# Norms of queries and keys: a maximum on VectorE and a power on GpSimd in place of Relu, Ln and Exp on ScalarE

## The chip, the core and the metric

The kernel runs on one NeuronCore of a Trainium2 chip. The metric is the device time of one launch in microseconds (us). The core has five engines with an instruction queue each, worked off in order: TensorE (PE, matmuls and transposes; PEld is its loading of weights), VectorE (DVE), ScalarE (ACT), GpSimd (POOL) and SyncE (SP, which here issues nearly all DMAs). All data are fp32.

## The reference

The input x is 4 sequences of 512 tokens with 128 channels. Six blocks follow each other, each with a layer norm ahead of it and a residual around it: a token-shift feed-forward block, global attention with 16 heads of 64 and a position bias, the feed-forward block again, then a two-layer local transformer, a gated linear recurrence, and the local transformer again with the same weights. What matters here is in the local transformer, in each of its two layers:

```python
def l2norm(t):
    return t / jnp.clip(jnp.linalg.norm(t, axis=-1, keepdims=True), 1e-12)

def _layer(x, wqkv, qs, ksc, wo, lg, lb, w1, b1, w2, b2):
    ...
    q, k, v = (to_heads(q), to_heads(k), to_heads(v))
    q = l2norm(q) * qs
    k = l2norm(k) * ksc
    q, k = rotary_xpos(q, k)
    o = local_attention(q, k, v)
    ...
...
x = x + 0.5 * _L1_ffn_ref(_layernorm(x, axis=-1), ...)
x = x + _L1_attn_ref(_layernorm(x, axis=-1), ...)
x = x + 0.5 * _L1_ffn_ref(_layernorm(x, axis=-1), ...)
```

A query or key of one head (64 numbers) is divided by its length. With 8 heads that makes 16 lengths per token. Local attention looks at windows of 64 tokens and the window before.

## The kernel before

The kernel does not write its instructions in the order in which they run. Every call on an engine is recorded first (`Recorder`, and `Plan.record`), with the tiles it reads and writes, a cost in us for the planner (`cost=` where the line gives one, else a formula in `Recorder.cost`), and a due time `plan.vt` that the program sets by hand. `Plan.plan` then walks through a model of the five queues: it takes, of the operations whose inputs are there, the one that can start first, and among those of nearly equal start the one with the earliest due time. It also hands out buffers: 33 pairs of 128x1040 floats in SBUF (each can be used as two halves), 24 small tiles of 128x16, 8 tiles for values, and 8 PSUM banks ("S"). It prices a change of the TensorE array shape and of ScalarE's function table: Exp and Ln are in one table, Gelu and Sigmoid in two others, and every change is an ACT_TABLE_LOAD (L288). `emit` writes the instructions in the planned order and pins that order on each queue. So all recorded instructions have line 318 in the profile, and groups are told apart by tile names: `pair` (halves and pairs), `small`, `psS` (PSUM), `xT` (a sequence, channels on partitions), `va` (values), `via` (a DRAM bounce buffer), and constants by their names, such as `tiny`.

A change of one cost therefore changes the order of much else: what follows in the plan, and which buffer each tile gets.

The work has three stages. The first feed-forward block runs over the 4 sequences. Global attention runs over 8 pairs of heads times 4 sequences, up to about 430 us. From there on, per sequence and overlapping each other in a staggered way: the second feed-forward block, `local_stage` (two layers), `recurrence`, `local_stage` again, `leave`.

`local_attention` works on 4 tiles of 128 tokens, pipelined by hand: in step k, `rotate(k)`, `values(k)`, `turn(k-2)`, `soften(k-3)`, `turn_back(k-5)`, `weigh(k-6)`, `turn_outputs(k-7)`, `project(k-8)`. There are 4 sequences x 2 stages x 2 layers x 4 tiles = 64 calls of `rotate`.

In `rotate` TensorE projects queries and keys (two matmuls of 512 columns), ScalarE squares them out of PSUM, and VectorE multiplies them out of PSUM by the cosine and the sine table into `u` and `w`. POOL adds the halves of the squares (L712), VectorE sums over each head into `rn`, a small tile of 128x16 (L713). Then comes the inverse length: L715 to L717, three ScalarE instructions on `rn`. POOL meanwhile adds the rotated halves of `w` to `u` (L718, L719, two instructions of 512 elements), and multiplies `u` by `rn`, spread over the 64 channels of a head (L721, 1024 elements). `turn` transposes that product for the attention matmuls: queries on TensorE, keys by 32x32 blocks on VectorE and through DRAM.

The three instructions compute exp(-0.5 ln(relu(s - 1e-24) + 1e-24)) for the sum of squares s, that is max(s, 1e-24) to the power of -1/2. The biases come from a constant tile `tiny` of two columns, set by two POOL memsets (L471 to L473).

Of the kernel before, what the change touches and what calls it, by code (L numbers as in the profile page):

```python
# [8 lines left out]
AF = mybir.ActivationFunctionType  # L9
ALU = mybir.AluOpType  # L10
# [4 lines left out]
P = 128  # L15
# [16 lines left out]
DEPTH, H1, DH, WIN = 2, 8, 64, 64  # L32
# [396 lines left out]
def tile_macaron(ctx: ExitStack, tc: tile.TileContext, i: dict, out: bass.AP):  # L429
# [6 lines left out]
    def real(name, shape, pool=pool):  # L436
        return pool.tile(shape, FP, tag=name, name=name)
# [11 lines left out]
    pe, dve, act, pool_, dma = plan.tensor, plan.vector, plan.scalar, plan.gpsimd, plan.sync  # L449

    def const(name, shape, space=pool):
        return plan.fixed(real(name, shape, space), shape)
# [15 lines left out]
    w_v = cload("w_v", [D, D], i["L0_ffn_W_v"])  # L468
    eps = const("eps", [P, 1])
    pool_.memset(eps, EPS)  # L470
    tiny = const("tiny", [P, 2])  # L471
    pool_.memset(tiny[:, 0:1], -1e-24)
    pool_.memset(tiny[:, 1:2], 1e-24)  # L473
    ones_sb = const("ones", [P, P])
    pool_.memset(ones_sb, 1.0 / D)

# [207 lines left out]
    def local_attention(l, h):  # L684
# [5 lines left out]
        def rotate(t):  # L690

            sq = plan.tile("pair", [P, 2 * INNER])
            u = plan.tile("pair", [P, 2 * INNER])
            w = plan.tile("pair", [P, 2 * INNER])
            u4 = u.rearrange("p (g h d) -> p g h d", g=2, d=DH)
            w4 = w.rearrange("p (g h d) -> p g h d", g=2, d=DH)
            for g in range(2):
                c = slice(g * INNER, (g + 1) * INNER)
                pq = plan.tile("S", [P, INNER])
                pe.matmul(pq, lhsT=h[:, t * P : (t + 1) * P], rhs=wqkv[:, c], start=True, stop=True)  # L700
                act.activation(sq[:, c], pq, AF.Square)
                p3 = pq.rearrange("p (h d) -> p h d", d=DH)
                for dst, tab in ((u, cs), (w, sn)):
                    dve.tensor_tensor(
                        dst[:, c].rearrange("p (h d) -> p h d", d=DH), p3,
                        tab[:, t, g].unsqueeze(1).to_broadcast([P, H1, DH]), ALU.mult,
                    )
            rn = plan.tile("small", [P, 2 * H1])

            s3 = sq.rearrange("p (h d) -> p h d", d=DH)  # L710
            sh = plan.tile("half", [P, 2 * H1, half])
            pool_.tensor_tensor(sh, s3[:, :, :half], s3[:, :, half:], ALU.add, cost=1.25)  # L712
            dve.tensor_reduce(rn, sh, AX.X, ALU.add)  # L713

            act.activation(rn, rn, AF.Relu, bias=tiny[:, 0:1])  # L715
            act.activation(rn, rn, AF.Ln, bias=tiny[:, 1:2])
            act.activation(rn, rn, AF.Exp, scale=-0.5)  # L717
            for lo, hi in ((slice(0, half), slice(half, DH)), (slice(half, DH), slice(0, half))):  # L718
                pool_.tensor_tensor(u4[..., lo], u4[..., lo], w4[..., hi], ALU.add, n=INNER)  # L719
            u3 = u.rearrange("p (h d) -> p h d", d=DH)  # L720
            pool_.tensor_tensor(  # L721
                u3, u3, rn.unsqueeze(2).to_broadcast([P, 2 * H1, DH]), ALU.mult, cost=1.87
            )
            us[t] = u
# [128 lines left out]
        def project(t):  # L853
# [9 lines left out]
            for rows_, cols in parts:  # L863
                c = slice(cols.start + t * P, cols.start + (t + 1) * P)
                dve.tensor_tensor(h[rows_, c], pj[rows_, :], h[rows_, c], ALU.add)


        order = (project, turn_outputs, turn_back, turn, values, rotate, soften, weigh)
        behind = {values: 0, rotate: 0, turn: 2, soften: 3, turn_back: 5, weigh: 6,
                  turn_outputs: 7, project: 8}  # L870
# [301 lines left out]
```

## Time and profile before

| | us |
|---|---|
| median of two runs (1146.81 and 1147.20) | 1147.01 |
| span of the profiled execution, first to last instruction | 1146.1 |
| busy: TensorE matmul | 1117.0 |
| busy: VectorE | 911.9 |
| busy: ScalarE | 877.0 |
| busy: GpSimd | 762.7 |
| Relu and Ln on the norms, 128 instructions, mean 309 ns | 39.6 |
| Exp on the norms, 64 instructions, mean 216 ns | 13.8 |
| function table loads, 54 instructions, mean 1283 ns | 69.3 |

The profiled execution has no time of its own beside its span; the two runs lie 0.7 and 1.1 us above that span. Busy time is the union of an engine's instructions; instructions of one engine can overlap a little, so the busy time of a group is less than its count times its mean. The idle time of a group is that of the engine just before its instructions, with the engine and the tile that ended it behind the arrow.

### The profile page before, as it was taken

How to read it: one execution, taken by the hardware profiler on the slowest of the kernel's cores; microseconds unless marked ns; L12 is line 12 of the kernel's file. 1: busy time of each engine (PE TensorE's matmuls, PEld its weight loads, DVE VectorE, ACT ScalarE, POOL GpSimd, SP SyncE). 2: the span in 40 equal slices, each digit the busy share in tenths (PEclk: the TensorE clock that was granted, in tenths of full speed). 3: DMA queues.
4: the chain of work that ended last, by engine and by line, in shares of the span. 5: the costliest groups of instructions: out<-in, count | busy, mean ns of one | idle time of the engine just before them, and what ended most of it. 6: DMA issues, size and time to landing. Idle time of an engine off the chain costs nothing.

```text
span 1146.1 us, 26884 instructions
## 1 busy us (share of the span) xinstructions
PE 1117.0 (97%) x9036; PEld 688.4 (60%) x9036; DVE 911.9 (80%) x2891; ACT 877.0 (77%) x1948; POOL 762.7 (67%) x575
## 2 busy tenths in 40 slices
PE   7999999999999999999999999999999999999997
PEld 3455656566655545557667666764457766666673
DVE  4787787868778779989788788867999978878863
ACT  5987777867787667878786788788887777777764
POOL 3675655656569459979776677523999867777610
PEclk9999999999999999999999999999999999999999
DMA  4379799797979744523432332300333423322310
GB/s 126 125 232 306 211 261 264 207 274 206 299 211 309 199 115 127 161 84 106 120 96 68 93 102 76 85 1 1 98 114 102 115 77 101 98 84 67 98 38 19
DMA packets 131613, 157.01 MB, mean 137 GB/s; under 512 B 15034, under 2 KB 101732, under 8 KB 131476
## 3 DMA queue, kind: packets, MB, share of 16 engines
q1 hardware_dynamic: 131188, 155.21, 46.4%
q8 instruction: 73, 1.20, 0.5%
q14 instruction: 64, 0.52, 0.2%
q10 hardware_dynamic: 288, 0.08, 0.0%
HBM read 78.39 MB, written 64.02 MB: 124 GB/s over the span
## 4 chain that ended last, share of the span: by engine, by line
PE 70%; DVE 13%; ACT 9%; issue 3%; POOL 2%; DMA 1%; SPq 0%; DVEq 0%; ACTq 0%; POOLq 0%
PE psS L318 70%; DVE pair L318 12%; ACT pair L318 7%; POOL pair L318 2%; DVE small L318 1%; ACT small L318 1%; DMA pair<-via 1%; ACT L288 1%; ACT va L318 1%; SPq L318 0%; DMA via<-pair 0%; DMA pair<-in_x_dram 0%; DVE xT L318 0%; DVEq L318 0%; ACTq L318 0%
## 5 line engine op out<-in xcount | busy, mean ns | idle before, releaser
L318 POOL TENSOR_TENSOR pair<-pair,small 128x1024 f32<-128x1024 f32 (+1 forms) x256 | 430.9, 1704 | 203.6 <-DVE small L318 127.7
L318 PE MATMUL psS<-pair,pair 64*64 64x128 f32 (+4 forms) x4544 | 372.5, 300 | 3.2 <-DVE small L318 1.3
L318 ACT ACTIVATE pair<-pair,small 128x128 f32<-128x128 f32 (+1 forms) x512 | 266.5, 553 | 91.7 <-DVE small L318 77.1
L318 PEld LDWEIGHTS psS<-pair,pair 128*64 128x64 f32 (+2 forms) x4544 | 252.6, 140 | 101.5 <-issue 31.3
L318 ACT COPY pair<-psS 128x512 f32<-128x512 f32 (+1 forms) x470 | 254.6, 593 | 63.5 <-PE psS L318 59.0
L318 POOL TENSOR_TENSOR pair<-pair,pair 128x512 f32<-128x512 f32 x166 | 215.2, 1309 | 109.1 <-ACT pair L318 66.8
L318 PEld LDWEIGHTS psS<-ident,pair 128*128 128x128 f32 x1488 | 171.2, 141 | 92.5 <-issue 69.9
L318 PE MATMUL psS<-ident,pair 128*128 128x128 f32 x1488 | 200.0, 275 | 9.2 <-DMA pair<-in_x_dram 5.5
L318 DVE CUSTOM_DVE_ANT_0 pair<-psS,pair 128x512 f32<-128x512 f32 x256 | 164.8, 679 | 37.1 <-PE psS L318 36.3
L318 PE MATMUL psS<-wqkv,pair 128*128 128x512 f32 x384 | 182.2, 598 | 3.4 <-DVE pair L318 3.0
L318 DVE STREAM_TRANSPOSE pair<-pair 128x512 f32<-128x512 f32 x208 | 142.8, 697 | 18.9 <-POOL pair L318 18.0
L318 POOL TENSOR_TENSOR pair<-pair 128x512 f32<-128x512 f32 x82 | 102.9, 1256 | 55.8 <-ACT pair L318 54.7
L318 PE MATMUL psS<-pair,w 128*128 128x512 f32 (+2 forms) x288 | 130.2, 595 | 0.4 <-POOL pair L318 0.2
L318 ACT ACTIVATE pair<-pair 128x512 f32<-128x512 f32 x152 | 94.5, 629 | 35.6 <-DVE pair L318 26.4
L318 DVE CUSTOM_DVE_ANT_0 pair<-psS,mask 128x128 f32<-128x128 f32 x512 | 113.9, 284 | 6.2 <-PE psS L318 4.8
L318 PE MATMUL psS<-pair 64*128 64x512 f32 x512 | 117.7, 601 | 0.0
L318 PEld LDWEIGHTS psS<-wqkv,pair 128*128 128x128 f32 x384 | 68.6, 190 | 74.6 <-issue 50.1
L318 DVE TENSOR_TENSOR pair<-psS,cos 128x512 f32<-128x512 f32 x128 | 87.2, 681 | 18.5 <-ACT pair L318 15.1
L318 DVE TENSOR_TENSOR pair<-psS,sin 128x512 f32<-128x512 f32 x128 | 87.2, 681 | 15.2 <-ACT pair L318 14.6
L318 ACT ACTIVATE pair<-psS 128x512 f32<-128x512 f32 x144 | 82.0, 596 | 18.6 <-PE psS L318 10.3
L318 PEld LDWEIGHTS psS<-pair,w 128*128 128x128 f32 (+2 forms) x288 | 50.7, 182 | 62.8 <-issue 49.5
L318 PEld LDWEIGHTS psS<-pair 64*128 64x128 f32 x512 | 48.5, 186 | 58.5 <-issue 42.0
(73 smaller groups left out, 1191.3 us busy)
## 6 DMA issues: line engine op xcount, KB each, us to landing
via<-pair SPq DMA_DIRECT2D x72, 512.0 KB, 3.8
pair<-via SPq DMA_DIRECT2D x288, 128.0 KB, 3.8
via<-pair SPq DMA_DIRECT2D x64, 256.0 KB, 2.1
pair<-via SPq DMA_DIRECT2D x256, 64.0 KB, 2.1
pair<-va SPq DMA_DIRECT2D x112, 130.0 KB, 2.3
table<-tdram SPq DMA_DIRECT2D x16, 511.5 KB, 7.2
pair<-table SPq DMA_DIRECT2D x16, 448.0 KB, 4.6
pair<-pair SPq DMA_DIRECT2D x48, 128.0 KB, 2.0
```

What stands on the lines that cost most here:

```text
L288: self.nc.scalar.add_instruction(mybir.InstLoadActFuncSet(name=self.nc.get_next_instruction_name(), engine=mybir.EngineType.Activation, ac ...
L318: real(*[a.resolve() if isinstance(a, View) else a for a in args], **{k: a.resolve() if isinstance(a, View) else a for k, a in kw.items()},)
```

## The change

The constant `tiny` gives way to a constant `power` of 128x16, filled with -0.5 by one POOL memset. In `rotate` the three ScalarE instructions give way to two: VectorE takes the maximum of `rn` and 1e-24, and GpSimd raises it, element by element, to the power in `power`. The planner is told 0.6 us for the power and its formula's value for the maximum.

```diff
@@ tile_macaron @@
-    tiny = const("tiny", [P, 2])
-    pool_.memset(tiny[:, 0:1], -1e-24)
-    pool_.memset(tiny[:, 1:2], 1e-24)
+    power = const("power", [P, 2 * H1])
+    pool_.memset(power, -0.5)
@@ rotate @@
             pool_.tensor_tensor(sh, s3[:, :, :half], s3[:, :, half:], ALU.add, cost=1.25)
             dve.tensor_reduce(rn, sh, AX.X, ALU.add)
 
-            act.activation(rn, rn, AF.Relu, bias=tiny[:, 0:1])
-            act.activation(rn, rn, AF.Ln, bias=tiny[:, 1:2])
-            act.activation(rn, rn, AF.Exp, scale=-0.5)
+            dve.tensor_scalar(rn, rn, 1e-24, None, ALU.max)
+            pool_.tensor_tensor(rn, rn, power, ALU.pow, cost=0.6)
             for lo, hi in ((slice(0, half), slice(half, DH)), (slice(half, DH), slice(0, half))):
                 pool_.tensor_tensor(u4[..., lo], u4[..., lo], w4[..., hi], ALU.add, n=INNER)
```

## The prediction

> **What bounds the kernel now.** I read the page first, then busy time by stretches, then the waits of single engines in those stretches, and last the instruction order of both kernels.
>
> ```profile
> span 1146.1 us, 26884 instructions
> PE 1117.0 (97%) x9036; PEld 688.4 (60%) x9036; DVE 911.9 (80%) x2891; ACT 877.0 (77%) x1948; POOL 762.7 (67%) x575
> ...
> POOL 3675655656569459979776677523999867777610
> ```
>
> TensorE (PE) is busy 97% of the span: only 29 us are left in which it stands still. That caps any gain from work on other engines. The POOL row says where another engine could take over: its digits are low in the first stage (the global attention) and 9 in the slices from about 430 to 545 us and from about 805 to 920 us. So I cut the local stage, which begins near 430 us, in four.
>
> ```profile
> core 0: us, PE busy (x) PEld busy (x) DVE busy (x) ACT busy (x) POOL busy (x), PEclk, DMA share, GB/s
> 430.00:545.00 115.00, 111.34 (x941) 68.05 (x940) 104.90 (x313) 92.14 (x211) 104.69 (x82) 1.00 0.40 120
> 545.00:805.00 260.00, 256.95 (x2479) 168.42 (x2478) 206.73 (x718) 206.49 (x425) 160.30 (x132) 1.00 0.24 71
> 805.00:920.00 115.00, 109.64 (x1087) 71.46 (x1087) 107.12 (x359) 93.72 (x223) 107.25 (x84) 1.00 0.38 109
> 920.00:1146.00 226.00, 217.65 (x2134) 143.78 (x2133) 165.87 (x605) 159.47 (x343) 126.33 (x102) 1.00 0.25 72
> ```
>
> The first and third rows are the dense stretches. In their 230 us PE has 9.0 us idle, POOL 18.1, DVE 18.0 and ACT 44.1. PE, POOL and DVE are all nearly full, ACT is the one with room. In the second and fourth rows PE is at 99 and 96%, and POOL has 199 us idle of 486. The granted clock is 1.00 in every row.
>
> The instructions that go, and the one that waits for them (groups of one shape):
>
> ```profile
> L318 ACT ACTIVATE small<-small,tiny 128x16 f32<-128x16 f32 x128 | 39.6, 309 | 37.2 <-DVE small L318 35.8
> ...
> L318 ACT ACTIVATE small<-small 128x16 f32<-128x16 f32 x64 | 13.8, 216 | 1.0
> ```
>
> The first group is the Relu and the Ln (two for each of 64 token tiles), the second the Exp. Between 430 and 1146 us, POOL and PE wait for them as follows (two lines from the waits of POOL, two from those of PE; columns: total us, times, longest):
>
> ```profile
> POOL pair L318 <- ACT pair L318: 90.5, 31, 17.6
> POOL pair L318 <- ACT small L318: 34.5, 23, 4.4
> ...
> PE psS L318 <- ACT pair L318: 3.4, 7, 0.7
> ...
> PE psS L318 <- ACT small L318: 0.8, 1, 0.8
> ```
>
> **What stays.** The order of both kernels is the same on PE up to the local stage; before it only two POOL memsets become one (a row of 0.10 us, within POOL idle at the start). So the first 430 us stay. From there the planner, given other costs, lays all queues out anew. The number of PE instructions is unchanged; 54 table loads stand on ACT before and after, so no table work is saved. No DMA is added, moved to another queue or dropped.
>
> **The change part by part, against the span of 1146.1 us** (0.9 under the median of 1147.0; I add 0.9 at the end).
>
> *ACT, three instructions less per tile.* 39.6 + 13.8 = 53.4 us of busy time go, and the 35.8 us for which ACT stood at the head of its queue waiting for the sum of squares. ACT has 164 us idle in these 716 us and is not the bound. What reaches the end is PE's own waiting for ACT: 3.4 + 0.8, and 0.4 for the copy of the values, 4.6 us. I take half: -2.3 us. Bounds: nothing, and -9.0, if all PE idle of the dense stretches were owed to a late ACT.
>
> *DVE, one maximum of 128x16 per tile.* No such row. The nearest are the reciprocals, 128x2 in 160 ns and 128x4 in 166 ns, and the accumulator read of 83 ns. I take 0.16 us: 64 x 0.16 = 10.2 us in all. Of 64 tiles, 27.5 have their norms in the dense stretches (26 and 29 Relu and Ln there, halved), so 27.5 x 0.16 = 4.4 us fall where DVE has 18.0 us free. Elsewhere DVE's idle of 113 us hides it. The maximum waits for the reduction on its own engine; in 15 tiles it follows it at once, and what queues behind it (PSUM evictions that PE waits for) stands for that wait; in the others one or more DVE instructions lie between, cover it, and make POOL wait longer. I take +0.7 us; bounds 0 and +4.4, with the cover gone.
>
> *POOL, one power of 128x16 per tile.* No row has this operation. From below: POOL's 128x1 multiply took 229 ns, and 15 more elements at the slope between its 128x512 and 128x1024 products by the norms, (1922 - 1048) / 512 = 1.7 ns, make 0.25 us. From above: a whole 128x1024 product, 1.92 us, that is 120 ns for each of 16 elements. The line carries the planner's figure 0.6; the same kind of figure for two other POOL lines, 1.87 and 1.25, stands beside rows of 1.92 and 1.31, within 5%. I take 0.6 us: 64 x 0.6 = 38.4 us. In the sparse stretches, 36.5 x 0.6 = 21.9 us lie in 199 us of idle and cost nothing. In the dense ones, 27.5 x 0.6 = 16.5 us meet 18.1 us of idle. Of these, 1.4 + 4.7 = 6.1 us were the wait for ACT's norm, which goes; the other 12.0 are waits for ACT's squares, DVE and PE, which stay. So 6.1 of the 16.5 are free and 10.4 press on a queue that would be 99% full (211.9 + 16.5 of 230). PE still draws on other batches there; I take half: +5.2 us. Bounds: 27.5 x 0.25 = 6.9 less 6.1, about +0.8; and 27.5 x 1.92 = 52.8 less 18.1, +34.7.
>
> What queues behind the power: in 48 of 64 tiles both additions of the rotated halves (1.31 us each) stand ahead of it and cover the reduction and the maximum, and the product by the norm comes next, which needs it anyway. The product now waits for POOL's own result; in the old trace a product starts as the additions end, without a visible gap, so I add nothing.
>
> On the choice of engine: the additions of 128x512 took 1.31 us on POOL, and two-input DVE products with both inputs in SBUF took 1.13 us for 64x512, a ratio of 1.16. [...]
>
> *PE's tile shapes change more often.* Counting runs of one array shape in the two orders, 195 become 208: 8 more of full shape, 5 of half or quarter. From the starts in the trace, 32 matmuls of 64x128 take 1.034 us and 64 take 1.907, so a run costs 2 x 1.034 - 1.907 = 0.161 us beyond its matmuls; a full-shape matmul before such a run holds the queue 0.094 us longer than its usual 0.110. So 5 x 0.161 + 8 x 0.094 = +1.6 us, on PE, hidden by nothing. Bounds 0 and +3.3 (13 x 0.25).
>
> Sum: -2.3 + 0.7 + 5.2 + 1.6 = +5.2; 1146.1 + 5.2 + 0.9 = 1152.2, rounded to **1152**. Beyond these terms the rearranged queues shift PE's idle time of 20.4 us in the local stage either way; I allow 9 us, its half in round figures.
>
> **Rivals.**
>
> *A cheaper norm path (faster, mostly within 2%).* ACT is freed on the path POOL and DVE wait on (DVE waits 45.9 us for ACT after 430 us), the planner uses it, and the dense stretches lose their PE idle: 1147.0 - 9.0 + 1.6 = 1139.6. For it: ACT's blocked 35.8 us. Against: PE waited for ACT only 4.6 us there, and the load goes to the two engines that are fuller. Over 2% faster means 23 us out of 20.4 of PE idle in the local stage, of which 8.4 lie after 920 us, mostly in the final drain: all but excluded unless matmuls that stand waiting behind each other's records are regained too.
>
> *The power is dear (slower).* In place of the Exp of L717, GpSimd needs t us for 16 powers. Once 27.5 t exceeds the 18.1 us idle, POOL sets the pace of the dense stretches, and PE, whose own work is unchanged, waits: the time is 1147.0 + 27.5 t - 18.1, plus 1.6. Slower than 2% (1170) from t = 1.5; at 1.92 it is 1183. For it: no row prices a power; POOL is at 91 and 93% there. Against: the line's 0.6.
>
> *The power blocks POOL's queue.* It waits for DVE's maximum, and if that comes late in the dense stretches by one DVE instruction of 0.68 us in each of 27.5 tiles, 18.7 us of POOL time are lost beside 16.5 of work: 35.2 - 18.1 + 1.6 = +18.7, 1165.7. Against: the covering additions in 48 tiles.
>
> **How the numbers follow.** Forecast (about 1142 to 1161): 0.57. Cheaper path (below 1142): 0.21, of which 0.04 beyond 2%. Blocked queue (about 1161 to 1170): 0.08. Dear power (above 1170): 0.14. Low end: 1132, where a tenth is left out, the forecast of the first rival less most of the 9 us; high end: 1174, t near 1.6. The bound of 2%, 1124 to 1170, is about what a measurement of this kernel can tell from no change. Faster 0.04, same 0.82, slower 0.14.
>
> **What would show it right or wrong.** A row of POOL powers x64 near 600 ns and DVE maxima x64 near 160; ACT busy near 824 us and POOL near 801; POOL above 97% busy in its two dense stretches, and PE idle there some 5 us longer; no POOL wait for ACT small in the local stage. PE idle smaller than before would refute the POOL term; powers over 1.5 us, or long waits of POOL for DVE small ahead of them, speak for the slower rivals.

## The result, and the profile after

The changed kernel takes 1267.16 us (two runs, 1264.96 and 1269.37) where the kernel before takes 1147.01: 1.104 times as long, 95% interval 1.1023 to 1.1058. The profiled execution spans 1263.2 us, 117.1 more than before. The prediction said 1152, with 1132 to 1174 as its range.

From the page of the changed kernel:

```profile
span 1263.2 us, 26806 instructions
PE 1158.3 (92%) x9036; PEld 704.5 (56%) x9036; DVE 951.3 (75%) x2955; ACT 842.8 (67%) x1756; POOL 944.6 (75%) x638
...
POOL 4667655655785699999889988229999989897920
...
L318 POOL TENSOR_TENSOR small<-small,power 128x16 f32<-128x16 f32 x64 | 187.8, 2934 | 7.6 <-DVE small L318 4.1
```

The last line is the power: 64 of them, 2934 ns each, 187.8 us in all. The busy rows say where it shows: POOL's busy time grew by 181.9 us, ScalarE's fell by 34, and TensorE, with the same 9036 instructions, has 104.9 us idle instead of 29.1. So 75.8 of the 117.1 us are TensorE standing still longer; for the other 41.3 it is busy longer with the same work, at a lower granted clock (the last section has the figures). The POOL row has turned to 8 and 9 over nearly the whole local stage, but for the slices around 820 us and the end.

On the chain of work that ended last, POOL's share went from 2% to 24% (the page before, then the page after):

```profile
PE 70%; DVE 13%; ACT 9%; issue 3%; POOL 2%; DMA 1%; SPq 0%; DVEq 0%; ACTq 0%; POOLq 0%
...
PE 47%; POOL 24%; DVE 14%; issue 6%; ACT 5%; DMA 3%; SPq 1%; POOLq 0%; DVEq 0%; ACTq 0%
```

The maximum, among the groups of VectorE:

```profile
L318 DVE TENSOR_REDUCE small<-pair 128x16 f32<-128x512 f32 x64 | 43.3, 677 | 22.6 <-POOL pair L318 22.6
L318 DVE TENSOR_SCALAR small<-small 128x16 f32<-128x16 f32 x64 | 41.9, 655 | 0.5
```

It takes as long as the reduction ahead of it, which reads 32 times as much. What PE waits for (us, times, longest; the first line is the local stage before, the others are the longest of the changed kernel):

```profile
PE psS L318 <- POOL pair L318: 0.2, 1, 0.2
...
PE psS L318 <- DVE pair L318: 33.8, 32, 3.6
PE psS L318 <- POOL pair L318: 30.1, 20, 6.0
PE psS L318 <- ACT pair L318: 15.4, 17, 2.3
```

Before, PE waited 0.2 us for POOL in the local stage; now 30.1 us, of which 23.7 us are transposes that wait for products by the norms. POOL's lateness also reaches PE through other engines: before its block transposes VectorE sat idle for POOL for 62.9 us, and for 18.0 us before the change.

### The profile page after: what moved, and what is told of

Read it like the earlier page. It is cut to its first block, busy times and chain, and to the rows that moved or that the text cites. A ratio compares the mean times of both kernels' runs of the same rounds, so it can differ in the third digit from the quotient of the medians.

```text
span 1263.2 us, 26806 instructions
## 1 busy us (share of the span) xinstructions
PE 1158.3 (92%) x9036; PEld 704.5 (56%) x9036; DVE 951.3 (75%) x2955; ACT 842.8 (67%) x1756; POOL 944.6 (75%) x638
## 4 chain that ended last, share of the span: by engine, by line
PE 47%; POOL 24%; DVE 14%; issue 6%; ACT 5%; DMA 3%; SPq 1%; POOLq 0%; DVEq 0%; ACTq 0%
PE psS L318 47%; POOL pair L318 16%; DVE pair L318 10%; POOL small L318 8%; ACT pair L318 4%; DVE small L318 3%; DMA pair<-via 1%; DMA via<-pair 1%; SPq L318 1%; DMA pair<-va 1%; DVE xT L318 1%; DMA pair<-in_x_dram 0%; DMA pair<-in_L_attn_wv_dram 0%; ACT L288 0%; POOLq L318 0%
## 5 line engine op out<-in xcount | busy, mean ns | idle before, releaser
L318 PE MATMUL psS<-pair,pair 64*64 64x128 f32 (+4 forms) x4544 | 382.1, 304 | 10.6 <-DVE pair L318 7.3
L318 PEld LDWEIGHTS psS<-pair,pair 128*64 128x64 f32 (+2 forms) x4544 | 257.1, 142 | 111.6 <-issue 28.1
L318 POOL TENSOR_TENSOR pair<-pair,pair 128x512 f32<-128x512 f32 x163 | 210.6, 1311 | 99.8 <-ACT pair L318 86.5
L318 PE MATMUL psS<-ident,pair 128*128 128x128 f32 x1488 | 215.3, 284 | 51.9 <-POOL pair L318 23.7
L318 PEld LDWEIGHTS psS<-ident,pair 128*128 128x128 f32 x1488 | 175.9, 145 | 151.6 <-issue 68.7
L318 PE MATMUL psS<-wqkv,pair 128*128 128x512 f32 x384 | 189.5, 617 | 13.5 <-DVE pair L318 7.6
L318 POOL TENSOR_TENSOR small<-small,power 128x16 f32<-128x16 f32 x64 | 187.8, 2934 | 7.6 <-DVE small L318 4.1
L318 DVE STREAM_TRANSPOSE pair<-pair 128x512 f32<-128x512 f32 x208 | 143.6, 700 | 64.0 <-POOL pair L318 62.9
L318 PE MATMUL psS<-pair,w 128*128 128x512 f32 (+2 forms) x288 | 132.9, 605 | 6.1 <-POOL pair L318 3.7
L318 POOL TENSOR_TENSOR pair<-pair 128x512 f32<-128x512 f32 x85 | 106.0, 1249 | 34.3 <-ACT pair L318 33.0
```

The lines of the kernel that those rows point to most:

```text
L318: real(*[a.resolve() if isinstance(a, View) else a for a in args], **{k: a.resolve() if isinstance(a, View) else a for k, a in kw.items()},)
```

## The experiments

Theory A: the power's time on GpSimd is the loss. The rivals: the maximum, which waits for GpSimd (B, later E); the new order of all queues (C); a plan made with a wrong cost (D).

**Four runs on the parts.**

```diff
# e1_cheap, from the changed kernel
-            pool_.tensor_tensor(rn, rn, power, ALU.pow, cost=0.6)
+            pool_.tensor_tensor(rn, rn, power, ALU.mult, cost=0.6)
# e2_honest, from the changed kernel
-            pool_.tensor_tensor(rn, rn, power, ALU.pow, cost=0.6)
+            pool_.tensor_tensor(rn, rn, power, ALU.pow, cost=2.93)
# e3_max, from the kernel before
-            act.activation(rn, rn, AF.Relu, bias=tiny[:, 0:1])
-            act.activation(rn, rn, AF.Ln, bias=tiny[:, 1:2])
+            dve.tensor_scalar(rn, rn, 1e-24, None, ALU.max)
+            act.activation(rn, rn, AF.Ln)
# e4_prices, from the kernel before, at its start (pbase filled with 0.37, pexp with -0.5)
+    for n, w in enumerate((1, 4, 16, 64)):
+        pool_.tensor_tensor(const(f"pw{n}", [P, P])[:, :w], pbase[:, :w], pexp[:, :w], ALU.pow, cost=3.0)
+    pool_.tensor_tensor(const("pwp", [P, 16])[:32, :], pbase[:32, :16], pexp[:32, :16], ALU.pow, cost=3.0)
+    pool_.tensor_tensor(const("pwone", [P, 16]), ones_sb[:, :16], pexp[:, :16], ALU.pow, cost=3.0)
+    pool_.tensor_tensor(const("pml", [P, 16]), pbase[:, :16], pexp[:, :16], ALU.mult, cost=0.3)
...
+    dve.tensor_scalar(const("vmx", [P, 16]), pbase[:, :16], 1e-24, None, ALU.max)
```

Expected of e1_cheap:

> The changed kernel with the power replaced by a product of the same two tiles, in the same order on every queue (the planner is told 0.6 us as before); the norms are then wrong in value, which no instruction's time depends on. Theory A (the power's 2.93 us on GpSimd is what costs): the product takes about 0.25 us, GpSimd's busy time falls by 64 x 2.7 = 172 us to some 772, and the time falls to 1145 to 1160. Rival B (the maximum on VectorE, which took 0.66 us on average and waits for GpSimd, is a large part): 64 x 0.5 us late, half of it felt, the time stays at 1165 to 1180. Rival C (the new order of the queues is bad by itself): the time stays above 1180.

Expected of e2_honest:

> The changed kernel with 2.93 us in place of 0.6 us as the planner's cost of the power, so that the queues are laid out for what it takes. Theory A (GpSimd has to carry 188 us more, and they stand in the chain from norm to product): GpSimd's busy time stays near 945 us, and the time stays above 1215. Rival D (most of the loss comes from a plan made for a power five times cheaper than it is): the sparse stretches, in which GpSimd had 199 us idle, take up the work and the time falls to 1165 to 1200.

Expected of e3_max:

> The kernel before with one part of the change alone: the maximum on VectorE in place of the Relu, then Ln and Exp on ScalarE as they were; no power. The maximum should again take 0.16 us where GpSimd runs nothing and up to 1.3 us where a GpSimd instruction with two inputs is running, 0.5 to 0.7 us on average. Theory A: this is a side cost, the time stays within 1140 to 1158. Rival B: 1160 to 1180.

Expected of e4_prices:

> The kernel before with powers of 1, 4, 16 and 64 elements on 128 partitions, 16 on 32 partitions, 16 of a base of 1/128, a product and a maximum of 16 elements, all on GpSimd in the first 30 us, and one maximum of 16 elements on VectorE; their results are not used. If the power is paid by the element: 0.4, 0.9, 2.9 and 11.5 us, that is (2.93 - 0.2) / 16 = 0.17 us an element, and 2.9 on 32 partitions. If it is a fixed cost of the call: all about 2.9. The product and GpSimd's maximum 0.2 to 0.3. The whole 1165 to 1175, since some 20 us come on GpSimd at the start.

Measured, with 1147.5 us for the kernel before on the same chip: e1_cheap 1172.0 us (1.0215, interval 1.02 to 1.023); e2_honest 1268.9 (1.1059, 1.1043 to 1.1076); e3_max 1174.1 (1.0228, 1.0211 to 1.0245); e4_prices 1156.6 in its one run.

The power takes 95 of the 120 us (1267.2 - 1172.0). A right cost for the planner recovers nothing, so rival D falls: POOL is busy for 946.1 us there, and the time is the same. But theory A is not all: 24.5 us stay in e1_cheap, and the maximum alone, in another order, gives 26.6. So rival B, the maximum, may be a part of the loss. The wrong values of the norms in e1_cheap do not show in the times of what is worked out from them: VectorE's block transposes take 698 ns there, 697 before the change and 700 in the changed kernel, its masked scores of 128x128 283, 284 and 283.

The price list (e4_prices, groups of POOL in the first 40 us; each ran once):

```profile
L318 POOL TENSOR_TENSOR pw<-pbase,pexp 128x64 f32<-128x64 f32 x1 | 10.5, 10543 | 0.0
...
L318 POOL TENSOR_TENSOR pwone<-ones,pexp 128x16 f32<-128x16 f32 x1 | 2.9, 2899 | 0.0
L318 POOL TENSOR_TENSOR pw<-pbase,pexp 128x16 f32<-128x16 f32 x1 | 2.9, 2897 | 0.0
L318 POOL TENSOR_TENSOR pwp<-pbase,pexp 32x16 f32<-32x16 f32 x1 | 2.9, 2891 | 0.0
L318 POOL TENSOR_TENSOR pw<-pbase,pexp 128x4 f32<-128x4 f32 x1 | 1.0, 1019 | 0.0
L318 POOL TENSOR_TENSOR pw<-pbase,pexp 128x1 f32<-128x1 f32 x1 | 0.6, 572 | 0.0
...
L318 POOL TENSOR_TENSOR pml<-pbase,pexp 128x16 f32<-128x16 f32 x1 | 0.2, 221 | 0.0
```

The power is paid by the element of a partition: from 1 to 64 elements (10543 - 572) / 63 = 158 ns each, on top of 0.41 us. The number of partitions (2891 ns on 32, 2897 on 128) and the base (2897 ns for 0.37, 2899 for 1/128) make no difference. A product of the same tiles takes 221 ns. The whole came out at 1156.6 where 1165 or more was expected, so only some 9 of POOL's 20 us at the start reached the end; why, the run does not show.

**Does the maximum wait for GpSimd?** VectorE and POOL of the changed kernel in the order of time (start, duration, in us):

```profile
576.46 0.69 DVE L318 TENSOR_REDUCE small<-pair 128x16 f32<-128x512 f32 x1 [0.54 <-POOL pair L318]
577.09 0.69 DVE L318 TENSOR_TENSOR pair<-psS,sin 128x512 f32<-128x512 f32 x1
577.70 1.22 DVE L318 TENSOR_SCALAR small<-small 128x16 f32<-128x16 f32 x1
578.84 0.68 DVE L318 TENSOR_TENSOR pair<-psS,cos 128x512 f32<-128x512 f32 x1
```

```profile
575.16 1.27 POOL L318 TENSOR_TENSOR pair<-pair 128x512 f32<-128x512 f32 x1
576.39 2.51 POOL L318 TENSOR_TENSOR pair<-pair,pair 128x512 f32<-128x512 f32 x2
579.00 2.91 POOL L318 TENSOR_TENSOR small<-small,power 128x16 f32<-128x16 f32 x1
```

The maximum starts at 577.70, just after POOL's second addition has begun, and ends at 578.92; the addition ends at 578.90. So it is in the whole trace: 11 of the 64 maxima took 158 to 196 ns, and of the 53 longer ones 52 end within 0.08 us of the end of a POOL instruction with two inputs, and the last one with a POOL memset. The additions that were to cover the chain are what holds it up: they stand ahead of the power in POOL's queue, and are running when the maximum comes.

The next four runs take this wait away without touching the order, and test order, chain and queue.

```diff
# e5_norelu, from the kernel before
-            act.activation(rn, rn, AF.Relu, bias=tiny[:, 0:1])
# e6_recip, from e3_max
-            dve.tensor_scalar(rn, rn, 1e-24, None, ALU.max)
+            dve.reciprocal(rn, rn)
...
-            act.activation(rn, rn, AF.Exp, scale=-0.5)
+            act.activation(rn, rn, AF.Exp, scale=0.5)
# e7_recip_pow, from the changed kernel
-    pool_.memset(power, -0.5)
+    pool_.memset(power, 0.5)
...
-            dve.tensor_scalar(rn, rn, 1e-24, None, ALU.max)
+            dve.reciprocal(rn, rn)
# e8_dead, from e1_cheap: a tile, and a power into it behind the product by the norms (L721)
+    dead = const("dead", [P, 2 * H1])
...
+            plan.ops[-1].calls.append(lambda: nc.gpsimd.tensor_tensor(
+                dead.resolve(), ones_sb[:, : 2 * H1].resolve(), power.resolve(), ALU.pow))
```

Expected of e5_norelu:

> The kernel before without the Relu, so Ln (with its bias of 1e-24) and Exp alone on ScalarE: the clamp becomes an addition of 1e-24, and the planner lays all queues of the local stage out anew, as in the changed kernel, with neither a maximum on VectorE nor a power. It is the control for the order. Theory E (the loss of 25 us in the runs with the maximum is the maximum's waiting for GpSimd): the time stays at 1140 to 1153. Rival C (any new order loses against the one the constants were set for): 1160 to 1180.

Expected of e6_recip:

> The run with the maximum alone, with VectorE's reciprocal of the same tile in the maximum's place in the same order, and +0.5 in the Exp (the clamp is left out). Reciprocals of small tiles took 0.16 us in every profile, whatever GpSimd ran. Theory E (the maximum's waiting for GpSimd costs the 25 us): 64 x 0.5 us of VectorE go, the time falls to 1145 to 1160. Rival C (order) and rival F (one more hop between engines in the chain, whatever its length): the time stays at 1165 to 1180.

Expected of e7_recip_pow:

> The changed kernel with the reciprocal in the maximum's place, in the same order, and an exponent of +0.5 (the clamp is left out). Theory A and E add up: some 20 us less than the changed kernel, 1240 to 1255. If GpSimd's queue sets the pace by itself, a VectorE that is 30 us freer changes nothing: 1262 to 1270.

Expected of e8_dead:

> The run with a product in the power's place, with one power of 128x16 on constants added to GpSimd's queue just behind each product by the norms, into a tile that nothing reads; the planner knows nothing of it. The power then takes GpSimd's time and stands in no chain of its own tile. If what costs is GpSimd's time (187 us more in its queue): within 15 us of the changed kernel, 1250 to 1275. If it is the 2.9 us in the chain from sum to product: 1172 to 1195.

Measured against 1147.55: e5_norelu 1153.5 us (1.0051, 1.0035 to 1.0068); e6_recip 1151.8 (1.0038, 1.0023 to 1.0053); e7_recip_pow 1264.6 (1.1019, 1.1002 to 1.1035); e8_dead 1269.9 (1.1071, 1.1051 to 1.1091).

```profile
L318 DVE RECIPROCAL small<-small 128x16 f32<-128x16 f32 x64 | 15.5, 243 | 0.6
```

That is e6_recip's line in the maximum's place: 243 ns, not 696 as in e3_max. The order is the same, and 22.3 us are gone (1174.1 - 1151.8). The two traces with the power, in one order, show the difference instruction by instruction: none of the 64 maxima of the changed kernel lies wholly inside a POOL instruction, while 41 of the 64 reciprocals of e7_recip_pow end 0.1 us or more before the POOL instruction that was running when they began, and all 64 take 208 to 254 ns, 244 on average. The kernel before shows the same of its own reciprocals, of 128x2 and 128x4: 186 of the 256 lie wholly inside a POOL instruction with two inputs, and these take 121 to 184 ns, 162 on average; the longest seen, 790 ns, is one of 128x4 in e3_max, where the median is 170. So the maximum's waiting costs 22 us in e3_max, and what remains over the kernel before, 4 us, is about what a new order costs without any such instruction (e5_norelu, 6 us, just outside the 1140 to 1153 expected). Beside the power the same swap is worth only 2.6 us (1267.2 - 1264.6), within the spread of the runs: there a VectorE that is freer changes next to nothing.

e8_dead decides between queue and chain. Its power is read by nothing and waits for nothing, and the product by the norms stands ahead of it; still the time is that of the changed kernel. What costs is the 187 us in POOL's queue, not the 2.9 us in the chain from sum to product.

**Four runs on the amount, the order, and what ScalarE's relief is worth.**

```diff
# e9_recip_cheap, from e1_cheap
-            dve.tensor_scalar(rn, rn, 1e-24, None, ALU.max)
+            dve.reciprocal(rn, rn)
# e10_half, from the changed kernel: in the power's place two instructions
+            plan.ops[-1].calls[:] = [lambda c=c, op=op: nc.gpsimd.tensor_tensor(
+                rn[:, c].resolve(), rn[:, c].resolve(), power[:, c].resolve(), op)
+                for c, op in ((slice(0, H1), ALU.pow), (slice(H1, 2 * H1), ALU.mult))]
# e11_drop, from the kernel before: planned, but not issued
             act.activation(rn, rn, AF.Relu, bias=tiny[:, 0:1])
+            plan.ops[-1].calls.clear()
# e12_noact: the same line behind the Relu, the Ln and the Exp
```

Expected of e9_recip_cheap:

> The changed kernel, in its order on every queue, with both prices taken out: the reciprocal (0.16 us) in the maximum's place, and a product (0.22 us) in the power's place; the norms are then wrong in value. It is the fourth corner beside the changed kernel (1267), reciprocal and power (1265), maximum and product (1172). If the maximum's waiting is worth as much in this order as in the other (22 us): 1148 to 1156, which is what my sum for the change would have been with the prices that it assumed. If the order is a part of the loss: 1160 to 1172.

Expected of e10_half:

> The changed kernel with the power on 8 of the 16 columns and a product on the other 8, issued together in the power's place, in the same order (half of the norms are wrong in value). The power of 8 should take 0.57 + 7 x 0.16 = 1.7 us, so GpSimd carries 64 x 1.7 = 109 us more than with the product alone, where the whole power makes 174 more and costs 95. If GpSimd's idle time takes up the first part and the rest is paid in full (174 - 95 = 79 us free): 1172 + 30 = 1202, range 1190 to 1212. If each us on GpSimd costs the same share (95 of 174): 1172 + 60 = 1232, range 1222 to 1240.

Expected of e11_drop:

> The kernel before, its planned order kept on every queue, with the Relu not issued (Ln's bias of 1e-24 alone keeps off zero). 20 us of ScalarE's work go and no order changes. If ScalarE's relief was worth something, as my sum had it (-2.3 us for three instructions): 1145 to 1147. If ScalarE's idle time hides it all: 1147 to 1148. If the queues, pinned in the old order, need the relief nowhere but the new start times collide: up to 1150.

Expected of e12_noact:

> The kernel before, its planned order kept, with none of the three ScalarE instructions issued: the product takes the sums as they come from VectorE (the norms are then wrong in value). All that the change takes away from ScalarE goes, and nothing is put elsewhere: the most that the change could have gained in this order. My sum said -2.3 us, with bounds of 0 and -9: 1138 to 1147. If the waits of GpSimd for ScalarE's norms (34.5 us) were on the path: below 1138.

Measured against 1147.51: e9_recip_cheap 1158.6 us (1.0098, 1.0081 to 1.0115); e10_half 1204.9 (1.05, 1.0475 to 1.0525); e11_drop 1144.9 (0.9977, 0.9968 to 0.9987); e12_noact 1147.7 (1.0006, 0.9993 to 1.0018).

e10_half answers the question of the amount. It fits "idle time first, then in full" (1202) and not "the same share of each us" (1232). By POOL's busy time (777.8 us in e1_cheap, 875.5 in e10_half, 944.6 in the changed kernel) the first 97.7 us cost 32.9, the next 69.1 cost 62.3. Two tables of stretches show the same, the first of e1_cheap, the second of the changed kernel:

```profile
core 0: us, PE busy (x) PEld busy (x) DVE busy (x) ACT busy (x) POOL busy (x), PEclk, DMA share, GB/s
430.00:750.00 320.00, 306.64 (x3032) 199.21 (x3031) 280.06 (x948) 220.40 (x446) 249.15 (x223) 0.99 0.34 100
750.00:800.00 50.00, 49.91 (x348) 30.45 (x349) 35.79 (x96) 40.28 (x67) 11.46 (x13) 1.00 0.01 1
800.00:1110.00 310.00, 294.42 (x2799) 189.32 (x2799) 270.31 (x900) 220.30 (x433) 244.63 (x219) 0.99 0.31 89
1110.00:1169.00 59.00, 51.88 (x464) 33.80 (x460) 28.89 (x112) 33.84 (x61) 7.44 (x7) 0.97 0.08 23
```

```profile
430.00:800.00 370.00, 327.96 (x3072) 208.73 (x3071) 288.06 (x973) 226.86 (x461) 334.25 (x226) 0.97 0.29 87
800.00:850.00 50.00, 47.87 (x318) 27.14 (x317) 33.45 (x74) 40.27 (x62) 11.19 (x12) 0.99 0.00 1
850.00:1200.00 350.00, 306.14 (x2700) 195.37 (x2699) 269.67 (x879) 213.59 (x421) 325.42 (x218) 0.94 0.27 77
1200.00:1263.00 63.00, 55.63 (x552) 36.50 (x550) 32.22 (x128) 36.32 (x64) 8.95 (x8) 0.99 0.10 31
```

The first and third row of each hold the two halves of the local stage that contain the norms. POOL's busy time there rises from 493.8 to 659.7 us, by 166. Its idle time falls from 136.2 to 60.3, which takes up 76, and the two stretches grow by 50 and 40 us, which is the other 90. At 90 and 93% busy, the idle time that POOL has left is nearly all waiting for its inputs. The holes, around 800 us and at the end (39 and 54 us of POOL idle after), took none of it: no norms fall there.

e9_recip_cheap came out between the two ranges expected of it. It closes the square of four in one order:

| us | reciprocal | maximum |
|---|---|---|
| product | 1158.6 | 1172.0 |
| power | 1264.6 | 1267.2 |

Read along the path from the kernel before: the new order and the small instructions 11.1, the maximum's waiting 13.4, the power 95.2; together the 119.7 us from 1147.5 to 1267.2. The shares depend on the path: with the reciprocal the power costs 106.0, and with the power the maximum 2.6. On either path the power is the bulk; the order is a smaller part, about as large as the maximum at its largest here.

e12_noact shows what the change could win in the old order: all three ScalarE instructions gone, nothing in their place, and the time does not move (1146.0 to 1152.3 in its ten runs). Dropping the Relu alone in the kept order (e11_drop) gives 2.6 us, and is the only version that beats both kernels; the same instructions in the order that the planner makes for them (e5_norelu) lose 6. Why the smaller relief gained and the larger did not, the runs do not settle.

## Why the prediction was wrong, point by point

**The power, the step that failed.** Its term was mis-sized: 0.6 us an instruction taken, 2.93 measured; +5.2 us in the sum, 95 to 106 us in the runs. Two things went wrong in it. I took 0.6 because the planner's figures on two other POOL lines agree with their rows; that a hand-written figure is right for two operations says nothing of a third that has never run. And the upper end, the 1.92 us of a 1024-element product, was no bound at all: it priced a power at 120 ns an element by taking it for cheaper than 64 products, and an element takes 158. A bound from the nearest row holds only for an operation of the same kind; for this one there was none, and the range should have stayed open above.

**The mechanism of the rival was right, and its formula too small.** "The power is dear" is what happened. Its formula with 2.93 gives 1147 + 27.5 x 2.93 - 18.1 + 1.6 = 1211, still 56 short. By the square, some 33 to 44 us of the 56 are the power's own (95 to 106 against the 62.5 of 27.5 x 2.93 - 18.1); the rest is the order and the maximum. The formula took all of POOL's idle time as usable and let the sparse stretches take up their 36.5 powers in 199 us of it. But 112 of the 199 lie where hardly a norm falls: 57.5 between 700 and 800 us, with 3.5 tiles, and 54.8 from 1080 us on, with none (the old trace in other stretches). And of the 136.2 us of idle time where the norms do fall, the power used 76 and left 60, nearly all of it waiting for inputs. Nor are dense and sparse places that stay: in the changed kernel both halves are dense.

**The maximum.** 0.16 us taken, with +0.7 us on the path and +4.4 at most; measured 0.66 us, and 13 to 22 us where the power is absent. The bare instruction was right (158 ns where POOL is between instructions). What I left out is that POOL's instructions hold up this one of VectorE's with no dependence between them: 53 of the 64 maxima took over 200 ns, up to 2250, and every one of these ended within 0.08 us of the end of a POOL instruction. The reciprocal in the same place does not show it (243 ns on average in e6_recip, 244 in e7_recip_pow). Why the one waits and the other does not, no run here shows.

**ScalarE's relief.** -2.3 us taken; 0.2 us the other way in e12_noact, within its interval of none, so PE's own waits for an engine, halved, were still too much; e11_drop gained 2.6 with the Relu alone. The 53.4 us that were to go from ScalarE's busy time were too many as well: it fell by 34.2 (842.8 instead of the 824 forecast), and by 37.3 in e12_noact. In the old trace the three groups overlap with other instructions of ScalarE, and without them its busy time would be 34.4 us less.

**The order and the tile shapes.** +1.6 us and 9 us either way. e9_recip_cheap, with both prices taken out, is at 1158.6. For its product of 0.22 us the prediction's working gives nothing on POOL (27.5 x 0.22 = 6.0 us, under the 6.1 free), so a sum of about 1147: the rest came out some 11 us above it, more than was allowed. e5_norelu and e6_recip, in other new orders, lost 6 and 4 us. So a new order cost more than the 1.6 us of the tile shapes; what in it costs was not separated.

**What was right.** The first 430 us stayed (in the new trace PE is busy for 420.7 of them). POOL stood at 97% in the first 115 us from 430 on (111.1 us), though not in the second dense stretch, which now holds the gap around 820 us (75.7 of 115). No wait of POOL for ACT's small tiles is left. The sign I listed for the slower rival, powers over 1.5 us, is the one that came.

## What to carry to other kernels

An operation that no row prices is an open risk on its engine's queue: measure it in a spare corner of the kernel, at two widths, before it goes on an engine whose idle time is a few tens of us. In this kernel, work moved to an engine that others wait for cost little while that engine had idle time in reach (a third of the first 98 us), and nearly all of itself afterwards; count that idle time only where the work can run. Here GpSimd held up VectorE with no dependence between them (53 of 64 maxima, at worst 2.25 us instead of 0.16): a small instruction that takes long, and ends with an instruction of the neighbour, shows it.

## What the runs showed of the hardware that was not expected

GpSimd's power costs 158 ns for each element of a partition beyond 0.41 us (e4_prices, 1 to 64 elements), 13 times a product of 16 (2897 against 221 ns), the same on 32 partitions as on 128 (2891 and 2897 ns). VectorE's maximum with a constant on 128x16 in SBUF takes 158 to 196 ns in the changed kernel when GpSimd is between instructions or just ending one, and up to 2.25 us when it is not; its reciprocal of the same tile takes 243 ns on average in e6_recip and 244 in e7_recip_pow, where 41 of 64 end while a GpSimd instruction is still running. In the two halves of the local stage, where TensorE was idle for longer, its granted clock was 0.97 and 0.94 instead of 1.00, and over the run its busy time rose by 41 us for the same matmuls (the projections of 512 columns from 598 to 617 ns). Which of these brings which, and how much of the 120 us that is, was not separated; between the two runs of the changed kernel, the longer one had the higher mean clock (0.980 at 1269.37 us, 0.975 at 1264.96).
